# Attention's gate at an earlier product, the last queries a unit sooner, and a second deferred seventh product

## The chip, the cores and the metric

The kernel runs on one core of a Trainium2 chip. The metric is device time in microseconds. Engines are named as in the profile: PE (TensorE, matmuls), DVE (VectorE), ACT (ScalarE), POOL (GpSimd), SP (SyncE, which issues most of the DMAs). Every engine takes its instructions in the order in which they stand in its queue.

## The reference

Eight sequences of 512 tokens with 576 features. First a rotation in a 64-dimensional subspace (QR of P, a matrix exponential per sequence), then one transformer block with adaptive norms. "Attention" is among the 16 heads of one token, not among tokens:

```
x_rot = x + ((x @ U) @ R - x @ U) @ U.T
ada = silu(c) @ ada_w + ada_b          # shift, scale, gate for attention and for the MLP
q, k, v = (modulate(layernorm(x)) @ qkv_w + qkv_b), reshaped to 16 heads of 36
attn = softmax(einsum('nthd,ntkd->nthk', q * scale, k))     # 16 x 16 per token
out = einsum('nthk,ntkd->nthd', attn, v).transpose(0, 2, 1, 3).reshape(n, t, d)
x = x + gate_msa * (out @ proj_w + proj_b)
x = x + gate_mlp * (gelu(modulate(layernorm(x)) @ fc1_w + fc1_b) @ fc2_w + fc2_b)
```

## The kernel before, in words

**Units.** A token tile is 128 tokens, so each of the 8 sequences (b) has 4 tiles. A unit is two tiles of one sequence, `(b, (0, 1))` or `(b, (2, 3))`; there are N = 16, numbered k = 0 to 15, and b = k // 2. After a prologue (QR, exponential, modulation, the first sequences' rotation), the loop at the end of the kernel goes over the units. In one pass it does, in program order:

1. `Projection(b, ts, gate_a)`: loads of the projection's weights, of attention's output for the two tiles (`at`) and of the residual rows (`x1`). Then `turn` (PE transposes, `atr`), `product` (four products `pj` of five matmuls, L957; DVE multiplies each by the gate, `pt` L959, and adds it to `x1`, L960) and `norm` (DVE statistics, POOL raises the variance to -0.5 in `rstd_m`, L146, DVE writes `xm` or `xn`, L147; POOL adds `gb2` to `x1`, L965). Among these stand the pieces of `qkv` for later tiles: six groups a tile, ten matmul rows a group (`qkvp`, L821), copied by ACT (`qs`, L832) and stored to DRAM (`tok`) from ACT's queue.
2. `turn_normed`: ten transposes (`h2tr`, L975) and ACT's modulation into `h2T` (L977).
3. `mlp`: five steps of fc1, for pairs of hidden groups g = (0, 1), (2, 3), (4, 5), (6, 7) and (8) (L1001), ACT's gelu (L1022), and fc2 one step behind. fc2 uses Strassen's scheme of seven products for the two tiles; POOL makes the sums `ss` (L1097 to L1099) and, for the seventh product, `s3s[g]` = first half minus second (L1100, `s<-gt`). The seventh product `p7` (L1106, 18 matmul rows) follows fc2's last step. DVE then puts the products together (`u`, L1121 to L1145), multiplies by the gate (`mt`, L1032) and POOL adds that to `x1` (L1033), which is stored.
4. In "aside" of the MLP's steps: the rotation of two tiles of sequence b + 2 (`rot` on PE, L762; `xt`, a norm with `rstd_a` on DVE and POOL), and its transposes (`htr`). Only units 0 to 11 have this.
5. `ops(40, att)`: the whole of attention for unit k + 1, which is DVE's work: per tile four products `qk` (L859) each with a reduction `sc` (L866), a softmax (L871 to L879, exp on ACT), four products `pv` (L887) each with a reduction `att` (L894), and a store to DRAM.

**What sets the order.** Only the prologue and the first unit's front are held to the program's order. Behind that a scheduler at build time places each engine's instructions: of those that its model of time says are ready, the first in program order. An engine then runs that fixed order. So attention, last in its pass, fills DVE's holes.

**The gate.** To keep attention from starting too soon, `attention(units[k + 2], after=...)` is made at the end of pass k. It begins with a copy of one column of `s3s[6]` of unit k's MLP into its score tile `sc[0]` (L852), so that no score of unit k + 2 can be reduced before POOL has made the s3 of group 6 in unit k. The first `qk` does not wait for it.

**The queries ahead.** `tiles_of` holds the 24 tiles of units 4 to 15. Passes k = 1 to 10 take two of them each, 11 to 14 one each, so that unit k + 3's tiles come in pass k up to unit 13, and the four tiles of units 14 and 15 in passes 11, 12, 13 and 14. For the last unit's attention (`apart`, k + 3 == N) the second tile's scores therefore stand behind the first tile's values.

**The deferred seventh product.** For k = N - 2 the MLP returns `rest`, and the seventh product, its two additions and the end of that unit's second tile run in the next pass, behind the projection's second norm. For the last unit the seventh product is done in two halves at the very end. `Projection.last` is set for the last unit: its first tile's two `pj` go to the PSUM pool `ps_mm` and not to the four banks of `ps_acc`, which fc2 holds.

Buffers that matter here: `qkv` tiles 3, `x1` 3, `gate1` and `gb2` one each, fc1's weights 4, fc2's and the projection's weights 3 of each kind.

The profile's line numbers are those of the kernel before; behind L903 the changed kernel's are 4 smaller.

Of the kernel before, what the change touches and what calls it, by code (L numbers as in the profile page):

```python
# [49 lines left out]
def rotate_then_dit_block(  # L50
# [25 lines left out]
    def tile_rows(a, t):  # L76

        return a.rearrange("(h t m) n -> t h m n", t=NT, m=M8)[t]
# [52 lines left out]
    def take(which):  # L131
        turn[which] += 1
        return rings[which][(turn[which] - 1) % len(rings[which])]
# [700 lines left out]

        return [lambda n=n: group(n) for n in range(6)]

    def attention(b, ts, after=None, apart=False):

        HC = 4
        hb = f"{b}_{ts[0]}"
        own = []
        for i in ts:
            if (b, i) not in toks:
                toks[b, i] = tiles.tile([128, 3 * D], F32, tag="qkv", name=f"qkv_{b}_{i}", bufs=3)
                nc.sync.dma_start(out=toks[b, i], in_=tok_d[b][i * 128 : (i + 1) * 128])
            own.append(toks.pop((b, i)))
        sc = [small.tile([128, H, H], F32, tag="sc", name=f"sc_{hb}_{t}", bufs=2) for t in range(2)]

        if after is not None:
            nc.vector.tensor_copy(sc[0][:, 0, 0:1], after())  # L852

        def scores(t):
            q = own[t][:, 0:D].rearrange("p (h d) -> p h d", d=DH)
            k = own[t][:, D : 2 * D].rearrange("p (h d) -> p h d", d=DH)
            for c in range(H // HC):
                pr = tiles.tile([128, HC, H, DH], F32, tag="pr", name=f"qk_{hb}_{t}_{c}", bufs=1)
                nc.vector.tensor_tensor(  # L859
                    pr,  # L860
                    q[:, c * HC : (c + 1) * HC].unsqueeze(2).to_broadcast([128, HC, H, DH]),
                    k.unsqueeze(1).to_broadcast([128, HC, H, DH]),
                    ALU.mult,
                )
                yield
                nc.vector.tensor_reduce(sc[t][:, c * HC : (c + 1) * HC, :], pr, AX.X, ALU.add)  # L866
                yield

        def raised(t):
            mx = small.tile([128, H], F32, tag="mx", name=f"mx_{hb}_{t}", bufs=2)  # L870
            nc.vector.tensor_reduce(mx, sc[t], AX.X, ALU.max)  # L871
            nc.vector.tensor_tensor(sc[t], sc[t], mx.unsqueeze(2).to_broadcast([128, H, H]), ALU.subtract)
            nc.scalar.activation(sc[t], sc[t], AF.Exp, scale=DH**-0.5)

        def shares(t):
            sm = small.tile([128, H], F32, tag="sm", name=f"sm_{hb}_{t}", bufs=2)
            nc.vector.tensor_reduce(sm, sc[t], AX.X, ALU.add)
            nc.vector.reciprocal(sm, sm)
            nc.vector.tensor_tensor(sc[t], sc[t], sm.unsqueeze(2).to_broadcast([128, H, H]), ALU.mult)  # L879

        def values(t):
            i = ts[t]
            v = own[t][:, 2 * D :].rearrange("p (d h) -> p d h", h=H)
            att = tiles.tile([128, H, DH], F32, tag="att", name=f"att_{hb}_{t}")
            for c in range(H // HC):
                pr = tiles.tile([128, HC, DH, H], F32, tag="pr", name=f"pv_{hb}_{t}_{c}", bufs=1)
                nc.vector.tensor_tensor(  # L887
                    pr,
                    sc[t][:, c * HC : (c + 1) * HC, :].unsqueeze(2).to_broadcast([128, HC, DH, H]),
                    v.unsqueeze(1).to_broadcast([128, HC, DH, H]),  # L890
                    ALU.mult,
                )
                yield
                nc.vector.tensor_reduce(att[:, c * HC : (c + 1) * HC, :], pr, AX.X, ALU.add)  # L894
                yield
            nc.sync.dma_start(
                out=att_d[b][:, i * 128 : (i + 1) * 128, :].rearrange("h t d -> t h d"), in_=att
            )


        yield from scores(0)
        raised(0)
        if not apart:  # L903
            yield from scores(1)
            raised(1)
        shares(0)
        yield from values(0)
        if apart:
            yield from scores(1)
            raised(1)  # L910
        shares(1)
        yield from values(1)

# [2 lines left out]
    class Projection:  # L916


        def __init__(self, b, ts, gate):
            hb = self.hb = f"{b}_{ts[0]}"  # L920
            self.b, self.ts, self.gate = b, ts, gate
            self.last = (b, ts) == units[-1]
            rows = att_d[b].rearrange("h (m t) d -> h m (t d)", t=TAU)
            self.at, self.aT, self.xn, x1s[hb] = [], [], [], []
            self.w = []
            for n in range(2):
                self.w.append([wst.tile([128, 3, HALF], F32, tag=k, name=f"{k}_p{hb}_{n}", bufs=3) for k in ("w2q", "w2t")])
                nc.sync.dma_start(out=self.w[n][0], in_=proj_w[n, :, 0:3])
                nc.sync.dma_start(out=self.w[n][1][:, 0:2], in_=proj_w[n, :, 3:5])
            for t, i in enumerate(ts):  # L930
                at = take("at")
                nc.sync.dma_start(out=at[:, 0:D], in_=rows[:, i * M8 : (i + 1) * M8, :])
                x1 = tiles.tile([128, D], F32, tag="x1", name=f"x1_{hb}_{t}", bufs=3)
                nc.sync.dma_start(out=x1, in_=tile_rows(xr_d[b], i))
                self.at.append(at)
                x1s[hb].append(x1)
# [120 lines left out]
    def mlp(pr, gate, aside):  # L1057
# [3 lines left out]
        gts, sums, s3s = {}, {}, {}  # L1061
# [45 lines left out]
            return ps  # L1107

        k = units.index((pr.b, pr.ts))
        if k < N - 2:  # L1110
            p7 = seventh(slice(0, HALF), "p7")

        def made(tag):
# [17 lines left out]
        nc.vector.tensor_tensor(u4, u4, p[2], ALU.add)  # L1131
        finish(hb, 0, 1, u4, gate)
        store(pr, 0)
        if k < N - 2:
            nc.vector.tensor_tensor(u2, u2, p7, ALU.add)
        c21 = made("u1")
        nc.vector.tensor_tensor(c21, u2, p[3], ALU.subtract)  # L1137
        if k == N - 2:
            c22 = made("u4")
            add(c22, u2, halves_of[5])  # L1140

            def rest():
                ps = seventh(slice(0, HALF), "p7")
                for n, c in enumerate((c21, c22)):
                    nc.vector.tensor_tensor(c, c, ps, ALU.add)  # L1145
                    finish(hb, 1, n, c, gate)
                store(pr, 1)

            return s3s, rest
# [19 lines left out]
    units = [(b, (i, i + 1)) for b in range(B) for i in (0, 2)]  # L1169
    N = len(units)  # L1170
# [22 lines left out]
    att = attention(*units[0])  # L1193
# [39 lines left out]
    att = attention(*units[1])  # L1233
# [2 lines left out]
    ahead = {0: q[2:]}  # L1236
    tiles_of = [(unit[0], i) for unit in units[4:] for i in unit[1]]
    for k in range(1, N - 1):
        for tile_ in [tiles_of.pop(0) for _ in range(2 if k < 11 else 1)]:
            ahead.setdefault(k, []).append(tile_)  # L1240
    assert not tiles_of
    gate_a = gate_m = gb2 = None
    for k, (b, ts) in enumerate(units):
        if ts[0] == 0:
            gate_a, gate_m = gate_rows(0, b), gate_rows(1, b)
            gb2 = big.tile([128, D], F32, tag="gb2", name=f"gb2_{b}")
            nc.sync.dma_start(out=gb2, in_=fc2_b.to_broadcast([128, D]))
            nc.gpsimd.tensor_tensor(gb2, gb2, gate_m, ALU.mult)
        pr = Projection(b, ts, gate_a)
        q = ahead.get(k, [])  # L1250
        if k:
            q = [piece for tile_ in q for piece in qkv(*tile_)]

        front = max(0, len(q) - 8)
        now(q[:front])
        pr.turn(0)
        now(q[front : front + 1])
        pr.product(0, 0)
        pr.turn(1)
        pr.product(0, 1)  # L1260
        pr.norm(0, gb2)
        pr.product(1, 0)
        pr.product(1, 1)
        pr.norm(1, gb2)
        if k == 0:
            ops(1, att)
        now(q[front + 1 : -1])
        if k == N - 1:
            rest()
        pr.turn_normed((0, 1))  # L1270
        now(q[-1:])
        pr.turn_normed((2, 3))
        pr.turn_normed((4,))
        if k == 0:
            held.close()
        aside = {}
        if b + 2 < B:
            if ts[0] == 0:
                coming = rotation(b + 2)
            p = coming[:3] if ts[0] == 0 else coming[3:]  # L1280
            aside = {1: p[0], 2: p[1], 3: p[2], 4: lambda: feature_major(b + 2, ts[0] // 2)}
        s3s, rest = mlp(pr, gate_m, aside)
        ops(40, att)
        if k + 2 < N:
            att = attention(*units[k + 2], after=lambda s=s3s[6]: s[:, 0:1], apart=k + 3 == N)


# [53 lines left out]
```

## Time and profile before

| what | value |
|---|---|
| median of 3 runs | 2158.01 us (2157.17 to 7304.47) |
| the profiled execution | 2156.77 us, of it 2155.1 in the span |
| instructions | 28246 |
| PE busy | 2051.7 us, 95% |
| DVE busy | 1818.1 us, 84% |
| POOL busy | 730.3 us, 34% |
| ACT busy | 432.9 us, 20% |
| HBM | 331.63 MB read, 58.94 MB written, 181 GB/s |
| chain that ended last | PE 75%, DVE 16% |
| one large DVE operation (128x2304) | 2.5 to 2.6 us; 512 of them |
| unit 8, first fc1 matmul to the next unit's | 116.1 us |
| units 11, 12, 13 | 104.1, 103.6, 103.0 us |
| units 14 and 15 | 86.3 us, and 74.8 to the end |

A row of a timeline gives the start, the duration, the engine, the line, the operation with its output and inputs, and in brackets how long the engine had stood before it and what it waited for. A row of a table of stretches gives each engine's busy time between two moments, then the clock that the throttle granted to PE (1.00 is full), the busy share of the DMA engines and their GB/s. In the list of waits stand the time in total, how often, and the longest.

### The profile page before, as it was taken

The numbers are of one execution on the slowest core, as the hardware profiler recorded it, in microseconds if no ns is written. First come the engines' busy times: TensorE is split into PE (matmuls) and PEld (weight loads), VectorE is DVE, ScalarE is ACT, GpSimd is POOL, SyncE is SP. The second block draws the span as 40 slices with busy tenths as digits, with TensorE's granted clock in tenths as the row PEclk, the third lists the DMA queues.
The fourth block names the chain that finished last, engine by engine and source line by source line (L and its number), as shares of the span: only waits on it lengthen the run. The fifth ranks groups of instructions, "written<-read, shape, count | busy, mean of one in ns | idle before, by whom it ended". The sixth has DMA issues, their size and how long they took to land.

```text
span 2155.1 us, 28246 instructions
## 1 busy us (share of the span) xinstructions
PE 2051.7 (95%) x10109; PEld 1621.1 (75%) x10109; DVE 1818.1 (84%) x2548; ACT 432.9 (20%) x1040; POOL 730.3 (34%) x959
## 2 busy tenths in 40 slices
PE   5996898999999999999999999999999999998998
PEld 3476666777878878887878787888878787776777
DVE  8898499799997988979797979798997999989821
ACT  2232222221211221222121121121121211111210
POOL 2331153241523333333333243323333434343322
PEclk9855799999999999999999999999999999999999
DMA  8202256375757666575748484756657676665564
GB/s 278 87 2 75 82 189 176 116 227 167 216 192 205 210 185 213 170 236 161 249 137 270 127 266 147 223 194 195 221 177 222 194 226 166 205 188 189 168 193 139
DMA packets 251456, 392.44 MB, mean 182 GB/s; under 512 B 86926, under 2 KB 139099, under 8 KB 251316
## 3 DMA queue, kind: packets, MB, share of 16 engines
q1 hardware_dynamic: 225396, 364.09, 54.9%
q10 hardware_dynamic: 25920, 26.55, 3.6%
q8 instruction: 80, 1.31, 0.2%
q14 instruction: 60, 0.49, 0.1%
HBM read 331.63 MB, written 58.94 MB: 181 GB/s over the span
## 4 chain that ended last, share of the span: by engine, by line
PE 75%; DVE 16%; issue 3%; POOL 2%; DMA 2%; ACT 2%; ACTq 0%; SPq 0%; POOLq 0%; DVEq 0%
PE fc L1001 25%; PE qkvp L821 15%; PE fc L1075 9%; PE fc L1080 6%; PE pj L957 5%; DVE sc L866 3%; PE fc L1077 3%; PE p L1106 2%; DVE qk L859 2%; PE ada L364 1%; PE rot L762 1%; PE zps L751 1%; DVE att L894 1%; DVE pv L887 1%; PE dp L282 1%
## 5 line engine op out<-in xcount | busy, mean ns | idle before, releaser
L1001 PE MATMUL fc<-h2T,w 128*128 128x256 f32 x2304 | 519.0, 381 | 3.4 <-ACT h2T L977 2.3
L821 PE MATMUL qkvp<-wqkv,hT 128*128 128x288 f32 (+1 forms) x1920 | 484.4, 409 | 7.5 <-ACT qs L832 5.3
L1001 PEld LDWEIGHTS fc<-h2T,w 128*128 128x128 f32 x2304 | 433.6, 191 | 70.9 <-ACT h2T L977 9.5
L821 PEld LDWEIGHTS qkvp<-wqkv,hT 128*128 128x128 f32 (+1 forms) x1920 | 363.0, 191 | 110.0 <-ACT qs L832 7.1
L859 DVE TENSOR_TENSOR qk<-qkv 128x2304 f32<-128x2304 f32 x128 | 336.7, 2631 | 4.2 <-ACT qkv L829 2.0
L887 DVE TENSOR_TENSOR pv<-sc,qkv 128x2304 f32<-128x2304 f32 x128 | 333.5, 2606 | 2.7
L894 DVE TENSOR_REDUCE att<-pv 128x144 f32<-128x2304 f32 x128 | 326.0, 2547 | 3.1
L866 DVE TENSOR_REDUCE sc<-qk 128x64 f32<-128x2304 f32 x128 | 326.2, 2548 | 2.5
L1100 POOL TENSOR_TENSOR s<-gt 128x128 f32<-128x128 f32 x144 | 88.9, 619 | 453.3 <-ACT gt L1022 453.3
L1022 ACT ACTIVATE gt<-fc,b 128x256 f32<-128x256 f32 x288 | 118.8, 471 | 610.1 <-PE fc L1001 575.2
L1075 PE MATMUL fc<-wq,gt 128*128 128x288 f32 x576 | 170.8, 417 | 9.9 <-ACT gt L1022 6.7
L1080 PEld LDWEIGHTS fc<-wt,ss 128*128 128x128 f32 x1152 | 161.2, 191 | 15.3
L1080 PE MATMUL fc<-wt,ss 128*128 128x144 f32 x1152 | 165.1, 287 | 0.0
L1033 POOL TENSOR_TENSOR x<-x,mt 128x288 f32<-128x288 f32 x64 | 71.6, 1120 | 227.3 <-DVE mt L1032 227.3
L832 ACT COPY qs<-qkvp 128x288 f32<-128x288 f32 x180 | 71.5, 397 | 378.4 <-PE qkvp L821 337.9
L1097 POOL TENSOR_TENSOR ss<-gt 128x128 f32<-128x128 f32 x144 | 116.9, 812 | 69.6 <-PE fc L1080 68.0
L1099 POOL TENSOR_TENSOR ss<-gt,ss 128x128 f32<-128x128 f32 x144 | 133.0, 924 | 10.0
L1075 PEld LDWEIGHTS fc<-wq,gt 128*128 128x128 f32 x576 | 99.4, 190 | 44.4 <-issue 15.6
L957 PE MATMUL pj<-w2q_p,aT 128*128 128x288 f32 x384 | 104.0, 406 | 2.9 <-DVE u L1137 1.6
L146 POOL TENSOR_TENSOR rstd_m<-rstd_m,mhalf 128x1 f32<-128x1 f32 x32 | 26.7, 835 | 222.1 <-DVE rstd_m L145 222.1
L1075 PE MATMUL fc<-wt,gt 128*128 128x288 f32 x288 | 93.9, 408 | 0.0
L1077 PE MATMUL fc<-wq,ss 128*128 128x288 f32 x288 | 93.9, 408 | 0.0
(265 smaller groups left out, 2379.9 us busy)
## 6 DMA issues: line engine op xcount, KB each, us to landing
w<-in_fc_w SPq DMA_DIRECT2D x288, 256.0 KB, 5.0
wq<-in_fc_q SPq DMA_DIRECT2D x144, 432.0 KB, 4.3
wt<-comb_d SPq DMA_DIRECT2D x144, 432.0 KB, 5.6
tok<-qs ACTq DMA_DIRECT2D x180, 144.0 KB, 1.8
qkv<-tok SPq DMA_DIRECT2D x30, 864.0 KB, 4.6
w2q_p<-in_proj_w SPq DMA_DIRECT2D x32, 432.0 KB, 4.0
xT<-in_x_t SPq DMA_DIRECT2D x16, 640.0 KB, 4.9
w1t<-in_fc_t SPq DMA_DIRECT2D x80, 128.0 KB, 4.4
```

The lines of the kernel that those rows point to most:

```text
L821: nc.tensor.matmul(ps, lhsT=hT[0:k, c, i * 128 : (i + 1) * 128], rhs=wqkv[0:k, c, cols], start=c == 0, stop=c == NK - 1,)
L859: nc.vector.tensor_tensor(pr, q[:, c * HC : (c + 1) * HC].unsqueeze(2).to_broadcast([128, HC, H, DH]), k.unsqueeze(1).to_broadcast([128, H ...
L866: nc.vector.tensor_reduce(sc[t][:, c * HC : (c + 1) * HC, :], pr, AX.X, ALU.add)
L887: nc.vector.tensor_tensor(pr, sc[t][:, c * HC : (c + 1) * HC, :].unsqueeze(2).to_broadcast([128, HC, DH, H]), v.unsqueeze(1).to_broadcast( ...
L894: nc.vector.tensor_reduce(att[:, c * HC : (c + 1) * HC, :], pr, AX.X, ALU.add)
L957: nc.tensor.matmul(ps, lhsT=aT[0:k, c, :], rhs=w, start=c == 0, stop=c == NK - 1)
L1001: nc.tensor.matmul(bank[:, k], lhsT=lhs, rhs=h2T[rows, c, 0 : NU * 128], start=start, stop=stop, skip_group_check=True)
L1022: nc.scalar.activation(gt[:, k].rearrange("p t s -> p (t s)"), bank[:, k], AF.Gelu, bias=b1[:, 2 * g + k : 2 * g + k + 1])
L1075: nc.tensor.matmul(p[k], lhsT=whole[k][0], rhs=whole[k][1], start=g == 0, stop=stop)
L1077: nc.tensor.matmul(p[2], lhsT=whole[2][0], rhs=whole[2][1], start=g == 0, stop=stop)
L1080: nc.tensor.matmul(bank[:, side], lhsT=lhs, rhs=rhs[:, n * QUARTER : (n + 1) * QUARTER], start=False, stop=stop, skip_group_check=True,)
L1099: nc.gpsimd.tensor_tensor(ss[:, 2], gt[:, 1, 0], ss[:, 1], ALU.subtract)
```

## The change

The gate of attention for unit k + 2 is opened by the s3 of an earlier group: `begin` is 6 for k up to 5, as before, then 5, 4, 3, 2, 1 for k = 6 to 10, and 0 for k = 11 to 13. Pass 11 takes two tiles of queries too, passes 12 and 13 one, pass 14 none; `apart` goes, as both tiles of the last unit are there in time. And the seventh product is deferred for k = N - 3 as well as for N - 2, so that unit 13's runs in pass 14 and unit 14's in pass 15; the last two units' projections use `ps_mm` for their first tile.

```
-    def attention(b, ts, after=None, apart=False):
+    def attention(b, ts, after=None):
...
         yield from scores(0)
         raised(0)
-        if not apart:
-            yield from scores(1)
-            raised(1)
+        yield from scores(1)
+        raised(1)
         shares(0)
         yield from values(0)
-        if apart:
-            yield from scores(1)
-            raised(1)
         shares(1)
         yield from values(1)
...
-            self.last = (b, ts) == units[-1]
+            self.last = (b, ts) in units[-2:]
...
         k = units.index((pr.b, pr.ts))
-        if k < N - 2:
+        later = N - 3 <= k < N - 1
+        if k < N - 3:
             p7 = seventh(slice(0, HALF), "p7")
...
-        if k < N - 2:
+        if k < N - 3:
             nc.vector.tensor_tensor(u2, u2, p7, ALU.add)
         c21 = made("u1")
         nc.vector.tensor_tensor(c21, u2, p[3], ALU.subtract)
-        if k == N - 2:
+        if later:
             c22 = made("u4")
             add(c22, u2, halves_of[5])
...
-        for tile_ in [tiles_of.pop(0) for _ in range(2 if k < 11 else 1)]:
+        for tile_ in [tiles_of.pop(0) for _ in range(2 if k < 12 else 1 if k < 14 else 0)]:
             ahead.setdefault(k, []).append(tile_)
     assert not tiles_of
-    gate_a = gate_m = gb2 = None
+    gate_a = gate_m = gb2 = rest = None
...
         now(q[front + 1 : -1])
-        if k == N - 1:
+        if rest:
             rest()
...
         if k + 2 < N:
-            att = attention(*units[k + 2], after=lambda s=s3s[6]: s[:, 0:1], apart=k + 3 == N)
+            begin = min(6, max(0, 11 - k))
+            att = attention(*units[k + 2], after=lambda s=s3s[begin]: s[:, 0:1])
```

## The prediction

> **What bounds the kernel now.** I read the page's busy times and its 40 slices first, then a table of stretches, one per unit, then what each engine waited for, and last the timelines of VectorE (DVE), GpSimd (POOL) and TensorE (PE) around one unit's start. A unit is two token tiles of a batch, numbered 0 to 15. F(k) is the start of unit k's first fc1 matmul, T(k) the end of the second "xm/xn" row (L147 with rstd_m) just before it.
>
> ```profile
> PE 2051.7 (95%) x10109; PEld 1621.1 (75%) x10109; DVE 1818.1 (84%) x2548; ACT 432.9 (20%) x1040; POOL 730.3 (34%) x959
> ...
> PE   5996898999999999999999999999999999998998
> ...
> DVE  8898499799997988979797979798997999989821
> ```
>
> PE is full from the fourth slice on, DVE is nearly so.
>
> ```profile
> core 0: us, PE busy (x) PEld busy (x) DVE busy (x) ACT busy (x) POOL busy (x), PEclk, DMA share, GB/s
> 1347.70:1463.80 116.10, 116.06 (x557) 94.16 (x557) 100.76 (x90) 23.39 (x53) 38.62 (x49) 1.00 0.64 200
> ...
> 1579.40:1683.30 103.90, 101.88 (x496) 82.55 (x496) 87.82 (x82) 21.01 (x47) 36.37 (x48) 1.00 0.68 215
> 1683.30:1787.40 104.10, 100.71 (x491) 81.53 (x491) 99.25 (x90) 20.55 (x45) 43.32 (x49) 1.00 0.67 200
> 1787.40:1891.00 103.60, 99.69 (x481) 80.39 (x482) 96.87 (x76) 18.30 (x41) 39.83 (x46) 1.00 0.68 199
> 1891.00:1994.00 103.00, 92.15 (x440) 74.03 (x438) 93.44 (x74) 16.18 (x36) 44.02 (x47) 0.96 0.62 186
> ```
>
> These are units 8 and 10 to 13, from F(k) to F(k+1). Up to unit 9 PE does 116 us of work in 116; from unit 10 on it idles 2, 3, 4 and 11 us. All that the change can win here is some 20 us, under 1%.
>
> ```profile
> 1126.17 0.45 POOL L1100 TENSOR_TENSOR s<-gt 128x128 f32<-128x128 f32 x1 [11.25 <-ACT gt L1022]
> ...
> 1135.39 0.91 POOL L1100 TENSOR_TENSOR s<-gt 128x128 f32<-128x128 f32 x1 [3.20 <-ACT gt L1022]
> 1137.07 0.45 POOL L1100 TENSOR_TENSOR s<-gt 128x128 f32<-128x128 f32 x1 [0.77 <-ACT gt L1022]
> ...
> 1165.37 0.45 POOL L1100 TENSOR_TENSOR s<-gt 128x128 f32<-128x128 f32 x1 [6.35 <-ACT gt L1022]
> ```
>
> ```profile
> 1159.05 0.58 DVE L147 TENSOR_SCALAR xn<-xt,mv_a,rstd_a 128x576 f32<-128x576 f32 x1 [0.66 <-POOL rstd_a L146]
> 1165.86 0.15 DVE L852 COPY sc<-s 128x1 f32<-128x1 f32 x1 [6.23 <-POOL s L1100]
> ...
> 1222.79 0.57 DVE L147 TENSOR_SCALAR xm<-x,mv_m,rstd_m 128x576 f32<-128x576 f32 x1
> ```
>
> This is unit 6, F = 1116.01. The gate is the copy L852: DVE takes its queue in order and stands 6.23 us until s3 number 6 is there. Then it works without a break to T(7) = 1223.36. The rows of s3 give each gate's time after F: number 6 at 49.8, 5 at 36.5, 4 at 34.7, 3 at 21.4, 2 at 20.3, 1 at 12.0, 0 at 10.6 (11.3 in units 11 to 13: 1683.34 to 1694.68).
>
> ```profile
> DVE sc L852 <- POOL s L1100: 44.2, 8, 6.2
> DVE xt L770 <- PE rot L762: 33.1, 5, 7.0
> ```
>
> This is DVE's waiting between T(6) and T(14), 883.6 us.
>
> **The gate.** The order in which the built programs' instructions stand on DVE tells what moves. At T(11) 18 large operations of attention (128x2304 multiplies and their reductions) more are done than before; at T(14) 12 more. That is 31 us of DVE's work (12 x 2.59) brought ahead of T(14). Behind T(14) DVE had room for it anyway: it stood 21.2 us for L1126 in unit 14 and 64.8 in unit 15. Before T(14) it had 92 us of waiting to fill. Whether it does is read from what stands between T(k) and the gate: 41 us of work in unit 6, 28 in 7, 21 in 8, but 5, 8, 0, 3 and 3 in units 9 to 13. There attention k+1 is finished when unit k's norm is, and the next may not start before s3, which itself comes from that norm: T, transposes, fc1, gelu, s3. So each unit from 9 to 13 is a ring on DVE: gate, its list of work, T, F, gate. The wait that was 6 us of slack becomes 10 to 22 us of path.
>
> The ring's length is F to gate, n large operations at 2.59 (start to start, 1168.63 to 1181.70 has this spacing), the small ones, 1.6 for waits on rstd and slower rows, then T to F. Small ones, by start-to-start times in the timeline: eight u/mt at 0.36, six half-width u at 0.21, twelve pt/x/stats at 0.36, two norms at 0.7, softmax 3.0: 13.0; each rotated tile behind the gate adds 2.15. The same count makes 49.7 of unit 12's stretch from gate to T (15 large ones; it took 50.9) and 47.1 of unit 10's (48.0). T to F is 5.0 where the projection's group stands between the transposes (1227.10 to 1232.04), 4.6 at unit 13, 3.0 at unit 14 with nothing between.
>
> Unit 6: 36.5 + 22 x 2.59 + 15.2 + 1.6 = 110.3 after F; PE comes to these transposes 111.1 after F (1227.10), so nothing is lost. Unit 7: 34.7 + 62.2 + 15.1 + 1.6 + 5.0 = 118.6 (before 115.7). Unit 8: 21.4 + 77.7 + 17.3 + 1.6 + 5.0 = 123.0 (116.1). Unit 9: 20.3 + 75.1 + 17.2 + 1.6 + 5.0 = 119.2 (115.6). Unit 10: 12.0 + 82.9 + 17.3 + 1.6 + 5.0 = 118.8 (103.9). Unit 11: 11.3 + 80.3 + 17.3 + 1.6 + 4.6 = 115.1 (104.1). Unit 12: 11.3 + 80.3 + 13.0 + 1.6 + 3.0 = 109.2 (103.6). Unit 13: 11.3 + 67.3 + 13.0 + 1.6 + 3.0 = 96.2 (103.0). Sum 800.1 against 761.9 (F(7) 1232.04 to F(14) 1993.95): +38.2.
>
> **The clock.** PE then waits for T about 7 us in unit 8, 3 in 9 and 10, some 9 in 12. What such a wait costs again afterwards:
>
> ```profile
> 1980.82 4.28 PE L821 MATMUL qkvp<-wqkv,hT 128*128 128x288 f32 x10
> ...
> 1993.95 9.36 PE L1001 MATMUL fc<-h2T,w 128*128 128x256 f32 x32 [0.20 <-ACT h2T L977]
> ...
> 2006.85 7.07 PE L1001 MATMUL fc<-h2T,w 128*128 128x256 f32 x32
> ```
>
> The granted clock was 0.58 from 1990 to 2000. After 2.64 us of idling ten matmuls took 4.28 (else 2.59), after 5.82 us the first 32 of fc1 2.29 too long, and these stand in the ring. I add 2.5 at unit 9's start, 1.2 (an even chance) at those of 10 and 11, 2.3 at 13's: 7.2. Unit 14's slow start is already in the old time behind F(14).
> The Trainium skill (TensorE: Matmul & The Clock Gate, Part 1: The HAM clock gate) says that the clock halves after an idle window of about 3.4 us and comes back after about 3.4 us of work. By that alone only units 9 and 13 would start slow, at 1.7 each, and the sum would be 4 lower, 2200; the row after 2.64 us of idling speaks for more, and the row decides.
>
> **The moved queries.** Thirty matmul pairs (60 rows, 14.57 us), six L832 copies at 0.4 on ACT and six tok stores on ACT's queue leave unit 14's front; unit 11's now has two tiles, those of 12 and 13 one each as before (a later one). Unit 10 to 11 then holds 101.9 + 14.6 = 116.5 of PE's work, below the ring's 118.8: cost 0 behind DVE, 12.6 by itself if the ring were shorter. Unit 13 to 14 falls to 77.6, and the ring of 96.2 keeps the 14.6 from being a gain. Attention 15 now finds both tiles; that "apart" goes only reorders it.
>
> **The second seventh product.** Eighteen matmuls (4.53) pass from ahead of projection 14 to behind it, where PE waits for T anyway: 0 here, -4.4 if PE were the bound. Its adds and mt (two rows each) stand ahead of unit 14's second norm and before T: counted in the 13.0. gate_7's load now follows them: 4.3 (1973.64) to land, gb 1.4 and two x adds 2.8 on POOL, so POOL is free about T + 9.5, before s3 number 0 at T + 13. SP's queue takes that load before x_7_2_0 and w_7_0_2_0, which is wanted at F + 10.7: 0, with about 3 us to spare. Projection 14 takes two banks of the other PSUM pool: 0, those are free by then.
>
> **SP's queue.** Attention's tile loads, its stores and the at loads behind them stand sooner among the weights. Each waits for DVE; in the list they lie 15 us or more ahead of what their followers are wanted for: 0, at worst some 5 in all. In unit 12 wq waits for a projection's buffer ahead of gate_6, and gb_6 is ahead of rstd on POOL: 1.5 (0.94 at 1773.09, 2.83 at 1979.95).
>
> Sum: 38.2 + 7.2 + 1.5 = 46.9. The profiled execution took 2156.77 (span 2155.1), 0.06% under the median 2158.01: 2203.7, I say 2204.
>
> **Rivals.** First, not slower: DVE keeps work in hand at the gates, so that nothing stands there. Then T(7) to T(14) is 228 x 2.59 + 110 + 11 = 712, and PE's own 742 (its busy time in the seven stretches) bounds: 20 us won, 2137. For it speaks that 92 us of waiting are there to fill; against it the 0 to 8 us of work between T and gate. It decides when the gates of units 8 to 13 wait under 31 us together; I count 22 + 10 + 17 + 13 + 15 with unit 8's 5: some 80. Second, slower, but within 2%: the ring stands, the clock holds, and the 1.6 is nearer 0 (unit 10 needed 0.9): 2203.7 - 7.2 - 1.5 - 11 = 2184 to 2201. Third, worse than the sum: SP's waits hold weights back (5), T to F is 5.8 as at 1677.55 (3), and every start is slow (8): 2204 to 2222. That the change does nothing is excluded by the order on DVE.
>
> **How the numbers follow.** About 2% (43 us, 2201) is what a measurement of this kernel can tell from no change. Forecast together with the third case, over 2201: 0.58. Second, 2184 to 2201: 0.34. First: 0.08, of which 0.02 for over 2% faster. So faster 0.02, same 0.40, slower 0.58. The range 2183 to 2222 leaves the first case and little else out.
>
> **What would show it.** L852's waits: near 20 us in unit 9 and 10 to 17 in units 10 to 13. The units from F to F: 123 and more in unit 8, near 119 in 9 and 10, 96 in 13. PE waiting for xm and a clock under 1 at the starts of 9 and 13. No wait of xt for rot. From F(14) on 161 us as before. It would be wrong if L852 waits little, or if DVE's stretches from gate to T come out shorter than counted.

## The result, and the profile after

| | before | after |
|---|---|---|
| median | 2159.45 us (4 runs, 2157.17 to 7304.47) | 2191.30 us (4 runs, 2182.61 to 2194.54) |
| ratio, 95% interval | | 1.0145 [1.0106, 1.0184] |
| profiled execution, its span | 2156.77, 2155.1 us | 2193.06, 2191.3 us |
| F(6) to F(7) | 116.0 us | 116.6 us |
| F(7) to F(14) | 761.9 us | 797.1 us |
| F(14) to the end | 161.1 us | 159.6 us |

The changed kernel is 1.45% slower; the ratio leaves out the one run of before that took 7304.47 us. The two profiled executions differ by 36.3 us: 35.2 in units 7 to 13, 0.6 in unit 6, -1.5 behind F(14), and 2.1 that are there before unit 6 (rounded each by itself). Those 2.1 are chance: F(6) lay between 1109.7 and 1118.2 us in the twelve profiled executions of this study, although the instructions up to there are the same in all of them, but for seven small DVE copies more in run 3. So kernels are best compared by their units.

In the page of the changed kernel the busy times, and the chain that ended last:

```profile
PE 2065.5 (94%) x10109; PEld 1629.5 (74%) x10109; DVE 1807.9 (83%) x2549; ACT 451.1 (21%) x1054; POOL 720.8 (33%) x959
...
PE 57%; DVE 28%; issue 6%; DMA 3%; POOL 3%; ACT 1%; SPq 0%; ACTq 0%; POOLq 0%; DVEq 0%
```

No engine does much more or less: ACT takes 18 us more, which are table loads (last section), and DVE's work even 10 us less. But its share of the chain went from 16% to 28%: the same work now lies where others wait for it.

Units 8 and 10 to 13 of the changed kernel, in the table of stretches:

```profile
core 0: us, PE busy (x) PEld busy (x) DVE busy (x) ACT busy (x) POOL busy (x), PEclk, DMA share, GB/s
...
1352.30:1476.70 124.40, 119.03 (x557) 96.36 (x558) 115.27 (x96) 26.26 (x55) 40.94 (x49) 0.97 0.67 199
...
1593.80:1712.20 118.40, 116.10 (x557) 94.03 (x557) 100.71 (x91) 27.12 (x56) 34.98 (x48) 1.00 0.71 206
1712.20:1827.20 115.00, 107.09 (x508) 85.95 (x508) 99.30 (x89) 24.03 (x49) 40.74 (x49) 0.97 0.62 180
1827.20:1934.50 107.30, 94.05 (x442) 75.42 (x440) 95.62 (x75) 19.04 (x38) 33.80 (x46) 0.93 0.60 179
1934.50:2031.80 97.30, 86.71 (x404) 69.71 (x403) 82.75 (x72) 17.79 (x35) 35.36 (x45) 0.92 0.58 175
```

Set against the rows of before, unit 8 grew from 116.0 to 124.3 with the same 557 matmul rows; PE stands 5 us in it. Units 11 to 13 have PE idle for 8, 13 and 11 us and a granted clock under 1.

What DVE waited for from F(6) to F(14), and three of the gates in its timeline:

```profile
DVE sc L852 <- POOL s L1096: 86.3, 8, 21.6
DVE xm L147 <- POOL rstd_m L146: 7.2, 10, 3.3
DVE xt L770 <- PE rot L762: 6.7, 1, 6.7
```

```profile
1373.88 0.15 DVE L852 COPY sc<-s 128x1 f32<-128x1 f32 x1 [5.65 <-POOL s L1096]
...
1496.54 0.15 DVE L852 COPY sc<-s 128x1 f32<-128x1 f32 x1 [21.55 <-POOL s L1096]
...
1946.61 0.15 DVE L852 COPY sc<-s 128x1 f32<-128x1 f32 x1 [12.64 <-POOL s L1096]
```

The waits for `rot` went from 33.1 to 6.7 and those at the gate from 44.2 to 86.3: DVE lost its slack and got a wait for its own norm's consequences. The three rows are units 8, 9 and 13, 21.6, 19.9 and 12.1 us after F.

Three of the starts in PE's timeline (units 9, 10 and 13), and the clock in the stretches around them and around F(12):

```profile
1469.99 0.48 PE L971 MATMUL h2tr<-ident,xn 128*128 128x128 f32 x1 [5.33 <-DVE xn L147]
...
1588.91 0.55 PE L971 MATMUL h2tr<-ident,xm 128*128 128x128 f32 x3 [1.36 <-DVE xm L147]
1589.29 2.59 PE L821 MATMUL qkvp<-wqkv,hT 128*128 128x288 f32 x10
...
1931.57 1.54 PE L971 MATMUL h2tr<-ident,xm 128*128 128x128 f32 x6 [9.05 <-DVE xm L147]
...
1934.49 9.92 PE L997 MATMUL fc<-h2T,w 128*128 128x256 f32 x32
```

```profile
1470.00:1476.00 6.00, 6.00 (x18) 4.84 (x19) 4.96 (x2) 2.75 (x6) 1.69 (x3) 0.51 0.91 246
...
1588.00:1594.00 6.00, 4.94 (x24) 3.48 (x25) 5.93 (x5) 2.69 (x6) 3.90 (x3) 1.00 0.35 96
...
1820.00:1827.00 7.00, 4.48 (x14) 3.66 (x15) 4.93 (x3) 2.48 (x6) 3.94 (x3) 0.54 0.82 169
...
1929.00:1935.00 6.00, 2.86 (x9) 2.01 (x10) 4.98 (x3) 2.29 (x5) 3.55 (x3) 0.50 0.36 52
```

The number after ACT and POOL is the granted clock. PE waits 5.33 us for DVE's norm and runs at 0.51 afterwards; after 9.05 us at 0.50, and the 32 fc1 matmuls take 9.92 us; after 1.36 us it stays at 1.00. The Trainium skill (TensorE: Matmul & The Clock Gate, Part 1: The HAM clock gate) puts the idle window at about 3.4 us; the rows shown here lie on both sides of it and agree. Two others do not: the row of before that the prediction weighed against it (2.64 us, and slow), and a wait of 2.58 us at 2010.8 in the changed kernel, with a clock of 0.66 in the 3 us behind it. What shorter waits do is taken up in the last section.

### The profile page after: what moved, and what is told of

Read it like the earlier page. It is cut to its first block, busy times and chain, and to the rows that moved or that the text cites. A ratio compares the mean times of both kernels' runs of the same rounds, so it can differ in the third digit from the quotient of the medians.

```text
span 2191.3 us, 28272 instructions
## 1 busy us (share of the span) xinstructions
PE 2065.5 (94%) x10109; PEld 1629.5 (74%) x10109; DVE 1807.9 (83%) x2549; ACT 451.1 (21%) x1054; POOL 720.8 (33%) x959
## 4 chain that ended last, share of the span: by engine, by line
PE 57%; DVE 28%; issue 6%; DMA 3%; POOL 3%; ACT 1%; SPq 0%; ACTq 0%; POOLq 0%; DVEq 0%
PE fc L997 17%; PE qkvp L821 13%; DVE sc L866 6%; PE fc L1071 6%; DVE qk L859 6%; PE pj L953 5%; DVE att L894 4%; PE fc L1076 4%; DVE pv L887 3%; PE p L1102 2%; PE fc L1073 2%; DMA w<-in_fc_w 1%; PE ada L364 1%; PE dp L282 1%; POOL rstd_a L146 1%
## 5 line engine op out<-in xcount | busy, mean ns | idle before, releaser
L1096 POOL TENSOR_TENSOR s<-gt 128x128 f32<-128x128 f32 x144 | 98.8, 690 | 431.1 <-ACT gt L1018 431.0
L1018 ACT ACTIVATE gt<-fc,b 128x256 f32<-128x256 f32 x288 | 118.4, 472 | 543.3 <-PE fc L997 512.9
L1029 POOL TENSOR_TENSOR x<-x,mt 128x288 f32<-128x288 f32 x64 | 67.2, 1051 | 251.7 <-DVE mt L1028 251.7
L1093 POOL TENSOR_TENSOR ss<-gt 128x128 f32<-128x128 f32 x144 | 111.9, 777 | 56.5 <-PE fc L1076 55.7
L1095 POOL TENSOR_TENSOR ss<-gt,ss 128x128 f32<-128x128 f32 x144 | 109.0, 757 | 10.0
L1124 DVE TENSOR_TENSOR u<-u,fc 128x288 f32<-128x288 f32 x16 | 7.2, 447 | 120.5 <-ACT u L1123 120.5
L953 PEld LDWEIGHTS pj<-w2q_p,aT 128*128 128x128 f32 x384 | 72.6, 194 | 29.5 <-DVE u L1128 5.5
```

Source lines behind the costliest of these rows:

```text
L953: nc.tensor.matmul(ps, lhsT=aT[0:k, c, :], rhs=w, start=c == 0, stop=c == NK - 1)
L1018: nc.scalar.activation(gt[:, k].rearrange("p t s -> p (t s)"), bank[:, k], AF.Gelu, bias=b1[:, 2 * g + k : 2 * g + k + 1])
L1093: nc.gpsimd.tensor_tensor(ss[:, 0], gt[:, 0, 1], gt[:, 1, 1], ALU.add)
L1095: nc.gpsimd.tensor_tensor(ss[:, 2], gt[:, 1, 0], ss[:, 1], ALU.subtract)
```

## The experiments

All in one table first, units from F to F in the profiled executions, in us. "Gate" is the change's falling gate, "queries" the moved tiles without `apart`, "seventh" the second deferred seventh product.

| kernel | 7 | 8 | 9 | 10 | 11 | 12 | 13 | 7 to 13 | 14 | ratio, 95% |
|---|---|---|---|---|---|---|---|---|---|---|
| before | 115.7 | 116.0 | 115.7 | 103.9 | 104.0 | 103.6 | 103.0 | 761.9 | 86.4 | 1 |
| after: gate, queries, seventh | 117.7 | 124.3 | 117.1 | 118.4 | 115.0 | 107.3 | 97.3 | 797.1 | 84.8 | 1.0145 [1.0106, 1.0184] |
| 1: queries, seventh | 115.7 | 116.0 | 115.7 | 116.2 | 104.0 | 101.9 | 93.2 | 762.7 | 85.7 | 0.9993 [0.9978, 1.0007] |
| 2: gate | 119.2 | 122.9 | 119.9 | 113.4 | 110.0 | 106.5 | 88.8 | 780.8 | 82.9 | 1.0073 [1.0047, 1.0100] |
| 3: after, gate at the norm | 117.6 | 123.3 | 115.7 | 122.3 | 105.5 | 104.7 | 93.3 | 782.3 | 84.2 | 1.0082 [1.0059, 1.0105] |
| 4: after once more | 117.6 | 124.4 | 117.2 | 118.3 | 115.3 | 107.2 | 97.2 | 797.2 | 84.8 | 1.0142 [1.0115, 1.0169] |
| 5: before, one gate | 115.7 | 127.3 | 115.7 | 103.8 | 105.1 | 103.5 | 102.7 | 773.7 | 87.0 | 1.0057 [1.0042, 1.0073] |
| 6: after, gate from group 5 | 115.7 | 116.0 | 115.7 | 116.0 | 106.1 | 100.3 | 94.5 | 764.3 | 86.9 | 1.0027 [1.0016, 1.0039] |
| 7: gate, queries | 117.6 | 124.2 | 117.2 | 118.3 | 114.6 | 106.4 | 104.6 | 802.8 | 85.3 | 1.0211 [1.0185, 1.0237] |
| 8: seventh | 115.7 | 116.0 | 115.7 | 104.2 | 104.0 | 101.9 | 99.1 | 756.6 | 87.4 | 0.9984 [0.9972, 0.9995] |
| 9: seventh, two gates at 5 | 116.2 | 116.1 | 115.7 | 103.9 | 104.9 | 98.7 | 96.9 | 752.4 | 87.5 | 0.9967 [0.9954, 0.9980] |
| 10: seventh, gates at 5 and 4 | 116.3 | 116.3 | 116.1 | 104.3 | 104.9 | 100.2 | 98.6 | 756.8 | 86.4 | 0.9970 [0.9959, 0.9981] |

Kernels 1 to 4 were timed against a before of 2156.39 us, 5 to 8 against 2154.62, 9 and 10 against 2156.92.

My theory is the ring of the prediction: a unit's length is the longest of PE's work, DVE's work from T to T, and the ring (F to gate, DVE's list from the gate to T, T to F). The rival is that the waits at the gate themselves, the transfers or the moved queries make the time. For the transfers the trace of the changed kernel is enough: from F(7) to F(14) PE waits 0.4 us for one and DVE 0.3, and the one that POOL waits for costs the 2.9 us told further below.

**1. The change without its gate.**

```
-            begin = min(6, max(0, 11 - k))
-            att = attention(*units[k + 2], after=lambda s=s3s[begin]: s[:, 0:1])
+            att = attention(*units[k + 2], after=lambda s=s3s[6]: s[:, 0:1])
```

> The changed kernel with the gate held at s3 number 6 everywhere, so that only the moved queries, the dropped 'apart' and the second deferred seventh product are left. Theory (the gate's ring on DVE costs all of it): unit 10 grows by the moved tile to 116.5 us, 11 and 12 stay near 104, unit 13 falls to 95 since its ring is 49.8 + 39 + 1.6 + 5; sum +5, so about 2162 us. Rival (the moved queries or the second deferred product cause the loss): 2185 to 2192 as the changed kernel.

2154.36 us, no different from before. Unit 10 takes the 12.3 us of the moved tile (PE busy 116.16 of 116.2 us) and units 12 and 13 give 11.5 of it back. I had expected 5 us more in the units and got 1; units 12 and 13 came some 2 us shorter each than expected. Queries and seventh product together, without the gate, cost nothing; the gate is needed for the loss.

**2. The gate alone.**

```
-            att = attention(*units[k + 2], after=lambda s=s3s[6]: s[:, 0:1], apart=k + 3 == N)
+            begin = min(6, max(0, 11 - k))
+            att = attention(*units[k + 2], after=lambda s=s3s[begin]: s[:, 0:1], apart=k + 3 == N)
```

> The kernel before with nothing but the earlier gates. Theory: units 7 to 9 as in the changed kernel (117.7, 124.3, 117.1), units 10, 11, 12 at 115.5, 110.5, 107.5 by their rings, unit 13 near 96 since attention 15 lacks its second tile and leaves DVE free; sum +27, so about 2184 us, with waits of L852 near 22, 10, 9, 13 and 15 us in units 9 to 13. Rival (the moved queries or the product cause the loss): 2157 to 2163.

2171.19 us: slower, but by some 16 us where I had expected 27. Units 7 to 9 are those of the ring. Unit 13 lasts 88.8 us for the 96 expected: attention 15 does not have its second tile there, less stands between the gate and T, and PE, busy for 85.1 us of it, is the bound instead of the ring. The gate of unit 11 waited 3.1 us where I had expected 9. So gate and rest cost 16 and -2 apart and 31 together (run 4): 17 us come only from both.

**3. The gate at the norm.** From unit 9 on attention k + 2 waits for a copy of one column of unit k's second norm.

```
+        mark = small.tile([128, 1], F32, tag="mark", name=f"mark_{pr.hb}", bufs=4)
+        nc.vector.tensor_copy(mark, pr.xn[1][:, 0:1])
...
-            att = attention(*units[k + 2], after=lambda s=s3s[begin]: s[:, 0:1])
+            gate = mark if k > 8 else s3s[begin][:, 0:1]
+            att = attention(*units[k + 2], after=lambda g=gate: g)
```

> The changed kernel, but from unit 9 on the gate is a one-column copy of the same unit's second norm instead of an s3, so that it opens at T and DVE never waits for fc1; attention runs ahead even further (no large operation is left behind T(14)). Theory (the wait in the ring costs the time, not the work brought forward): units 9 and 10 at PE's 116.5, 11 at 104.5, 12 at 101.5, 13 at 96, units 7 and 8 as in the changed kernel; about 2172 us and no L852 wait from unit 9 on. Rival (attention's large operations among the norm's cost it, whatever the gate): 2190 or more.

2172.33 us, the number expected, in part by luck: unit 10 came 6 us longer than expected and unit 12 3 us longer, unit 13 3 us shorter. What DVE waited for from F(9) to F(14):

```profile
DVE pt L955 <- PE pj L953: 24.1, 8, 12.0
DVE xm L147 <- POOL rstd_m L146: 6.9, 9, 2.0
```

No L852 is left, and DVE now waits for PE. With the way through fc1, gelu and s3 out of the ring, units 9 and 11 to 13 fall from 437 to 419 us (before 426). Unit 10 is longer instead, 122.3 for 118.4: PE works 117.5 us in it and stands 2.4 for a transpose of the rotation and 2.2 for a gelu. Why this order brings those two waits is open.

**4. The changed kernel again.**

> The changed kernel once more, for a second profile beside the first. Its four times lie between 2182.6 and 2194.5 us, and the granted clock falls as the time rises (0.960 to 0.954). Theory: the ring's waits of L852 are the same to 1 us, and what differs is how many units start at the reduced clock after PE's waiting. Rival: the waits themselves differ, by DMA or by DVE's rows.

2187.29 us. Units 7 to 14 and the gates' waits in them came back within 0.3 us, and the same units started slow; unit 6 was 0.6 us shorter. What else differs between the two executions lies ahead of F(6) (1115.0 here, 1118.1 in the first profile). For these two, my guess that a varying number of slow starts makes the spread falls; the other executions of this kernel have no profile.

**5. One gate, early and never waited at.**

```
-            att = attention(*units[k + 2], after=lambda s=s3s[6]: s[:, 0:1], apart=k + 3 == N)
+            begin = 0 if k == 8 else 6
+            att = attention(*units[k + 2], after=lambda s=s3s[begin]: s[:, 0:1], apart=k + 3 == N)
```

> The kernel before, with one gate changed: in unit 8 attention waits for s3 of group 0 instead of group 6; nothing else. DVE's order then holds 129.3 us of work between T(8) and T(9) (43 large operations instead of 32), all of it in front of unit 9's transposes, and the gate stands behind 23.9 us of work, so s3 number 0 is there long before. Theory (what counts is the work that stands in DVE's queue ahead of the norm, and not the waiting at the gate): no wait at unit 8's gate, unit 8 lasts 128 to 131 us instead of 116.0, then unit 9's gate waits some 35 to 40 us, unit 9 lasts 115.5 to 116 and nothing comes back: 2168 to 2172. Rival (the cost is the waiting at the gate; work without a wait is only done sooner, and comes back): unit 8 at most 119, or the loss returned by unit 13: 2155 to 2160.

The gate of unit 8 in DVE's timeline, the unit and the next one in the table of stretches, and DVE's waits in that next one:

```profile
1362.08 2.67 DVE L887 TENSOR_TENSOR pv<-sc,qkv 128x2304 f32<-128x2304 f32 x1
1364.67 0.14 DVE L852 COPY sc<-s 128x1 f32<-128x1 f32 x1
1364.78 2.55 DVE L894 TENSOR_REDUCE att<-pv 128x144 f32<-128x2304 f32 x1
```

```profile
1349.90:1477.20 127.30, 119.03 (x556) 96.17 (x556) 125.49 (x100) 25.93 (x55) 46.67 (x49) 0.97 0.64 194
1477.20:1592.90 115.70, 114.71 (x549) 92.38 (x548) 75.11 (x80) 22.84 (x51) 34.85 (x50) 1.00 0.61 185
```

```profile
DVE xt L770 <- PE rot L762: 32.2, 2, 20.6
DVE sc L852 <- POOL s L1100: 6.2, 1, 6.2
```

There is no bracket behind the gate: nothing was waited for. DVE works 125.5 of 127.3 us, and the unit is 11.3 us longer than before, the largest loss of any unit 8 here. Unit 9 has 38.4 us of waiting, most of it not at the gate, where I had expected it, but for the rotation, and is no longer and no shorter than before. This is the plainest run of the study: DVE was idle for 1.8 us in all, everything that it did was needed some time, and it cost 11 us, because eleven large operations more than before, which nobody wanted yet, stood in front of a norm that PE wanted at once (43 for 32). (Unit 8 came out 0.7 us and the total some 3 us under my lower figures.)

**6. The gate held at group 5.**

```
-            begin = min(6, max(0, 11 - k))
+            begin = min(6, max(5, 11 - k))
```

> The changed kernel, with the gate held at group 5 from unit 6 on instead of falling to group 0; the queries and the second seventh product as in the change. Theory: DVE has 28 us of work from T to the gate, so the gate waits about 13 us in units 7 to 10, in each of them longer than in most of the changed kernel's; but gate to T is 72.1 us by count and the ring 115.2, under PE's 116 us: units 7 to 9 stay at 115.5 to 116.5, unit 10 is 116 to 117 by PE, 11 is 108 to 110, 12 is 103 to 105, 13 is 94 to 97; together 2162 to 2168. Rival (waiting at the gate costs by its length, or any earlier gate costs in proportion to the groups that it is earlier): units 7 to 9 at 118 or more, 2172 to 2185.

Units 7 and 8 in the table of stretches, and DVE's waits in units 7 to 9:

```profile
1232.50:1348.20 115.70, 114.71 (x550) 92.43 (x549) 98.99 (x90) 25.40 (x53) 39.49 (x50) 1.00 0.64 198
1348.20:1464.20 116.00, 115.99 (x557) 94.09 (x557) 98.93 (x90) 25.90 (x55) 38.07 (x49) 1.00 0.64 200
```

```profile
DVE sc L852 <- POOL s L1096: 23.7, 3, 7.9
DVE xt L770 <- PE rot L762: 20.5, 3, 7.1
```

Here DVE waits 14.7 us in each unit, 7.9 of it at the gate (I had expected 13 there), and none of the three is longer than before. By itself this says little against the rival, since the same two waits made 12.7 us a unit in the kernel before (6.2 at the gate). It does show that a gate one group earlier costs nothing here. The rival about the waits is settled by run 5: no wait and 11 us lost in unit 8, 38 us of waits and nothing lost in unit 9. In the changed kernel itself the longest wait at a gate, 21.6 us in unit 9, goes with 1.5 us more than before. What decides is whether DVE's list reaches T before PE does. Units 11 and 12 came 2 to 3 us shorter than I expected, and with them the total.

**7. The change without the second deferred seventh product.**

```
-            self.last = (b, ts) in units[-2:]
+            self.last = (b, ts) == units[-1]
...
-        later = N - 3 <= k < N - 1
-        if k < N - 3:
+        later = k == N - 2
+        if k < N - 2:
...
-        if k < N - 3:
+        if k < N - 2:
             nc.vector.tensor_tensor(u2, u2, p7, ALU.add)
```

> The changed kernel without the second deferred seventh product: gates and queries as in the change, only the last but one unit's seventh product deferred, as before. Theory (the 17 us by which gate and rest together cost more than the two apart come from the moved queries, which put attention's second tile of the last unit into unit 13's ring and one more large operation into unit 10's): units 10 to 12 as in the changed kernel (118, 115, 107), unit 13 by the ring's count 105.2, measured 101 to 105 instead of 97.3, unit 14 about 86: 2188 to 2196. Rival (they come from the second seventh product, whose sums and whose later projection 14 sit in the ring): units 11 to 13 as with the gate alone (110, 106.5, 89 to 92), 2172 to 2178.

2197.89 us, 2 us over the upper figure. Units 7 to 12 are those of the changed kernel within 1 us, so it is the queries, set behind the early gates, that make the 17 us that gate and rest cost only together. Against the gate alone (run 2) unit 10's list from gate to T counts 100.2 us instead of 97.6, unit 11's 97.6 instead of 93.3, and unit 13's 88.1 instead of 50.3, as attention 15 is there whole; the units are 4.9, 4.6 and 15.7 us longer. Unit 13 is 104.6 us by the ring's count of 105.2, with DVE full but for the gate and PE idle for 18:

```profile
1923.90:2028.50 104.60, 86.33 (x403) 69.41 (x402) 90.75 (x74) 17.91 (x34) 38.33 (x48) 0.89 0.55 168
```

The second deferred seventh product takes 7.3 us out of that unit. The gate and T(14) on DVE without it (run 7):

```profile
1935.01 0.15 DVE L852 COPY sc<-s 128x1 f32<-128x1 f32 x1 [11.60 <-POOL s L1096]
...
2024.95 0.57 DVE L147 TENSOR_SCALAR xm<-x,mv_m,rstd_m 128x576 f32<-128x576 f32 x1
```

One of the product's two sums and T(14) with it (the changed kernel; the gate, at 1946.61, is shown further above):

```profile
2026.01 0.44 DVE L1142 TENSOR_TENSOR u<-u,p 128x288 f32<-128x288 f32 x1
...
2027.76 1.04 DVE L147 TENSOR_SCALAR xm<-x,mv_m,rstd_m 128x576 f32<-128x576 f32 x1 [0.44 <-POOL rstd_m L146]
```

From gate to T it is 90.5 us without the deferral and 82.2 with it. The product's own sums do not make the difference, since in the changed kernel they still stand ahead of T. What leaves the list is three of attention's large operations (29 without, 26 with), 7.8 us. Why the scheduler places them behind the norm once PE's 4.5 us stand later is not shown.

**8. The seventh product alone.**

> The kernel before with the second deferred seventh product alone. Theory: unit 13 is bound by DVE's ring behind its gate at group 6, 104.1 by count, and the product's two sums leave it: 100.5 by count, 99 to 100 measured instead of 103.0; what PE has less in unit 13 it has more in unit 14, 86.4 to 88: 2153 to 2157, within 0.2% of the kernel before. Rival (unit 14 takes all 4.5 us of the product onto the path): 2156 to 2160.

Its edit is the plus and minus lines of run 7 turned round, and `if rest:` in the loop. 2150.70 us, ratio 0.9984 with an interval that ends at 0.9995: a small gain, larger than expected, 3.9 us in unit 13 as expected and 1.6 in unit 12, of which unit 14 takes 1.0 back. In unit 13 gate to T falls from 52.3 to 44.6 us, and F to gate and T to F take 3.7 of that back.

**9 and 10. The seventh product with two gates, of units 12 and 13 alone.**

```
+            begin = {12: 5, 13: 5}.get(k, 6)
```

> The kernel before with the second deferred seventh product, and only the gates of units 12 and 13 at group 5 instead of 6. Theory: from T to T DVE then has 99.7 and 94.2 us of work in units 12 and 13 (98.5 and 90.2 without the two gates), gate to T is 53.6 and 49.2 by count, the rings 96.7 and 92.3, so the gates stop binding and unit 12 lasts about 102 (DVE full), unit 13 about 96 instead of 99.1 with the product alone, unit 14, with two large operations less, 86 to 87 instead of 87.4: 2145 to 2151, a little under the product alone. Rival (any earlier gate costs, as in the changed kernel): unit 13 at 100 or more, 2152 or more.

> As the run before, with unit 13's gate at group 4: gate to T 51.8 by count with s3 number 4 at F + 34.7, DVE's work from T to T the same 94.2. Theory: DVE is full either way, so the same within 1 us: unit 13 about 96, 2145 to 2151. Rival (earlier costs more): unit 13 2 us or more longer than with group 5.

Run 10 has `{12: 5, 13: 4}`. 2150.30 and 2150.26 us: 0.9967 [0.9954, 0.9980] and 0.9970 [0.9959, 0.9981] of the kernel before. In run 9, units 12 and 13 in the table of stretches, and both gates in DVE's timeline:

```profile
1788.20:1886.90 98.70, 95.12 (x463) 76.87 (x463) 97.12 (x76) 17.62 (x39) 38.27 (x46) 1.00 0.67 196
1886.90:1983.80 96.90, 93.69 (x457) 76.20 (x456) 89.59 (x72) 18.35 (x39) 35.00 (x44) 1.00 0.69 195
```

```profile
1826.92 0.14 DVE L852 COPY sc<-s 128x1 f32<-128x1 f32 x1
...
1926.31 0.14 DVE L852 COPY sc<-s 128x1 f32<-128x1 f32 x1
```

Neither gate is waited at, PE is idle for 3 to 4 us in each unit and its clock stays at 1.00. So an earlier gate is no loss where it only fills DVE's holes. These are the best kernels of the study, though their interval overlaps that of run 8, so that what the two gates add to the seventh product (4.3 us by the units of run 9, 0 by those of run 10) is not settled. Nor are 9 and 10 told apart: their medians agree, while run 10's profiled execution is 0 to 1.7 us longer in each of units 7 to 13. Of that 1.7 are in unit 13, but 1.5 are in unit 12, whose gate is the same in both, so the rival of run 10 (earlier costs more) stays open.

## Why the prediction was right in kind and 13 us too high

The forecast of 2204 us held in its mechanism and lay 13 us over the measured median; it also gave the greater chance to over 2%, and 1.45% came. Against the profiled execution its 46.9 us split up like this: units 7 to 13 measured 11.7 less than forecast (797.1 for 800.1 and the 8.7 of clock and POOL), unit 6 0.6 more, F(14) to the end 1.5 less, the start 2.1 more: 46.9 - 11.7 + 0.6 - 1.5 + 2.1 = 36.4, the 36.3 up to rounding.

**The ring: right.** Units 7 to 13 were forecast at 118.6, 123.0, 119.2, 118.8, 115.1, 109.2, 96.2 and came at 117.7, 124.3, 117.1, 118.4, 115.0, 107.3, 97.3. The gates' waits in units 8 to 13 were forecast at 5, 22, 10, 17, 13, 15 and came at 5.7, 21.6, 9.3, 15.9, 11.6, 12.6. By stretches, clock and POOL's term lying in the measured ones:

| seven units together | forecast | measured |
|---|---|---|
| F to gate | 122.3 | 118.9 |
| gate to T | 647.2 | 644.4 |
| T to F | 30.6 | 33.8 |

**F to s3 number 0: mis-sized, -5.7.** I took 11.3 from the rows of before. In units 11 and 12 it was 9.4. Unit 11 on ACT and on POOL, first before, then after:

```profile
1691.65 1.28 ACT L1022 ACT_TABLE_LOAD   x1 [7.91 <-PE fc L1001]
1692.95 1.57 ACT L1022 ACTIVATE gt<-fc,b 128x256 f32<-128x256 f32 x4
```

```profile
1693.50 1.18 POOL L1100 TENSOR_TENSOR s<-gt 128x128 f32<-128x128 f32 x1 [14.29 <-ACT gt L1022]
```

```profile
1720.52 1.57 ACT L1018 ACTIVATE gt<-fc,b 128x256 f32<-128x256 f32 x4 [7.93 <-PE fc L997]
```

```profile
1721.07 0.46 POOL L1096 TENSOR_TENSOR s<-gt 128x128 f32<-128x128 f32 x1 [13.77 <-ACT gt L1018]
```

Both wait for fc1 equally long (F is 1683.34 and 1712.19). Then ACT loaded a table for gelu before, since attention's exp had come in between; afterwards no exp does, as all of attention's softmax lies between the gate and T, and the 1.28 us are gone: the gelu starts 9.61 us after F with the load and 8.33 without. The Trainium skill (ScalarE: Activation LUTs, What ACT_TABLE_LOAD costs) counts a drain of 1.38 us besides; none of it shows on this path. And POOL's own row takes 0.46 us instead of 1.18 while DVE stands; before, DVE was in a two-input multiply (1691.81 to 1694.37; more such rows in the last section). In unit 13 the interval was 12.1, which is 9.4 and the 2.7 of the slow clock (9.92 us for the 32 fc1 matmuls instead of 7.17). I had taken an interval from a kernel in which other work lay around it, and the change itself moves that work.

**The clock: mis-sized, 4.4 for 7.2.** 1.7 at unit 9 (T to F 6.7 for 5.0; forecast 2.5), 0 at 10 and 11 (forecast 1.2 each, with PE waiting 3 us; it waited 1.36 us and not at all), 2.7 at 13 (2.3). F(12) started at 0.54 as well, after 4.64 us, which I had not foreseen; T to F was 4.7 for the forecast 4.6 all the same, since only six instead of ten query matmuls stood among those transposes. The step that failed is the even chance at F(10) and F(11).

**Gate to T: mis-sized, -5.7.** That is 644.4 less the 2.9 of POOL's term, against 647.2. The 1.6 us for waits and slower rows were too much; 0.9, which unit 10 of before had needed, would have been the better row. Run 5 says the same: 127.3 where the count said 129.3 and more.

**The POOL term: 1.5, and 2.9 came.** It came in unit 11's stretch, on POOL by the mechanism that the prediction named. POOL's rows and then DVE's:

```profile
1807.02 1.40 POOL L1245 TENSOR_TENSOR gb<-gb,gate 128x576 f32<-128x576 f32 x1 [6.11 <-DMA gate<-gates_d]
1808.37 0.55 POOL L146 TENSOR_TENSOR rstd_m<-rstd_m,mhalf 128x1 f32<-128x1 f32 x1
```

```profile
1808.96 0.58 DVE L147 TENSOR_SCALAR xm<-x,mv_m,rstd_m 128x576 f32<-128x576 f32 x1 [3.32 <-POOL rstd_m L146]
```

gb_6 stands ahead of rstd in POOL's queue and waits for its load; DVE's norm waits 3.32 us where 0.4 is usual. What held the load back in SP's queue is only in part what I had named: wq waited 0.5 us there for the projection's buffer, the load of x ahead of it 2.7 for a store to land, and the store behind it 1.3 for POOL.

**T to F(11): +1.5, not foreseen.** T(11) lay at 1705.7, and PE, full with queries, came to the transposes at 1707.24. The terms together: -5.7 - 2.8 - 5.7 + 1.4 + 1.5 = -11.3 for the -11.7 measured; the other gates, 0.4 us sooner after F in all, are the rest.

**The moved queries: 0, right, with the bound right too.** Forecast 0 behind the ring and 12.6 by themselves; run 1 shows 12.3 in unit 10. What the text did not say is that the ring of unit 13 is as long as it is because of them: without them (run 2) the unit lasts 88.8 us and PE bounds it.

**The second seventh product: "0 here" was wrong as the price of that part.** In unit 13 it saves 7.3 us in the changed kernel (run 7) and about 4 alone (run 8), through DVE's list; from F(7) to the end it is 6.1 and 4.2. The ring's 96.2 had that in it, as it counts the 26 large operations that are left, so the sum was not touched.

**The rivals.** The first (not slower) needed waits at the gates under 31 us; 76.7 came. (The 742 that it gives PE in the seven stretches are 739.8 in the trace, which changes nothing here.) Even with short waits it would have failed, as run 5 shows: its condition named the waits, and the waits are not what counts. The second (the ring holds, with smaller margins, 2184 to 2201) is where the measured time lies, through the margins (-5.7, -5.7) more than through the clock (-2.8). But for the POOL term, SP's queue cost nothing that the waits show.

## What to carry to other kernels

On an engine that takes its instructions in order, work done sooner is paid for by whatever stands behind it. Before a gate is opened earlier, count the list between the gate and the next result that another engine wants: F to gate, the list, and back to F. If that ring is longer than the other engine's work, every unit pays the difference, with or without a visible wait; if shorter, the earlier gate is free and may fill holes, as in runs 6 and 9. Count the engine's whole work from one such result to the next as well: in run 5 that, with no wait at the gate, made unit 8. And price a part in the kernel as it will be: in unit 13 the seventh product was worth 4 us before the change and 7 within it.

## What the runs showed of the hardware

- From F(6) to F(15), over all twelve profiled executions, every wait of PE of 2.99 us or more was followed by a granted clock of 0.50 to 0.73 over the next 3 us. Waits up to 1.6 us that began at full clock left it at 1.00, where no longer wait came right behind them. Between the two it went either way: 1.00 after 2.71 us in run 9, 0.66 after 1.86 us in the same run. So the length of the wait alone does not decide it there, and what does is open. The same wait for the norm ahead of unit 8 in run 2 and in run 4, each with its stretch of 3 us behind it (the clock is 0.62 and 1.00):

```profile
1341.99 0.33 PE L975 MATMUL h2tr<-ident,xm 128*128 128x128 f32 x1 [1.68 <-DVE xm L147]
1342.00:1345.00 3.00, 3.00 (x10) 2.24 (x11) 2.97 (x2) 1.02 (x2) 1.60 (x2) 0.62 0.44 54
```

```profile
1343.70 0.33 PE L971 MATMUL h2tr<-ident,xm 128*128 128x128 f32 x1 [1.67 <-DVE xm L147]
1343.70:1346.70 3.00, 3.00 (x15) 2.42 (x16) 2.97 (x2) 1.02 (x2) 1.60 (x2) 1.00 0.52 59
```

- POOL's 128x128 subtractions (s3) took 0.46 us in the median where DVE stood or was in no two-input operation (115 of the 144 rows of the kernel before, at most 0.67), and 2.45 us in the median where DVE was in a two-input operation for over 80% of the row (10 rows, 0.46 to 2.69).
- ACT's table loads at exp and at gelu went from 34 to 48 (17 to 24 at each, 1.28 us apiece): the 14 instructions and nearly all of the 18 us that ACT is busier. More loads in all, but none in the two intervals that stood on the path of units 11 and 12.
- Start to F(6) varied by up to 8.6 us from run to run of equal code, while units 7 to 14 of the changed kernel repeated within 0.3 us. A comparison under 0.4% needs the units, or many runs.
